# A graph network of four layers on one core: table rows two blocks later, GAT weights prepared at other places, sums of attention weights by halves

## The chip, the cores and the metric

The kernel runs on one core of a Trainium2 chip. The metric is the device time of one execution in microseconds (us), the median of three runs. The engines are called PE (TensorE, matrix products), DVE (VectorE), ACT (ScalarE), POOL (GpSimd, which here also issues the gathers) and SP (SyncE, which issues DMAs). Each engine works through its own instructions in order; semaphores hold an instruction until what it reads is there.

## What is computed

Eight batches of 2048 nodes with 128 features go through four layers. All four use the same random adjacency matrix, in which about 16 of 2048 entries of a row are set.

```python
def reference(x, adj, ...):
    x = graph_attention(adj, x, L0)     # layers 0 and 1: 8 heads of 16
    x = graph_attention(adj, x, L1)
    x = gat(x, adj, L2)                 # layers 2 and 3
    return gat(x, adj, L3)

def graph_attention(adj, h, w):
    Q, K, V = h @ Wq, h @ Wk, h @ Wv                      # per head
    attn = softmax(where(adj == 0, -inf, Q K^T / 4))
    x = layer_norm(h + (attn V) @ Wo + bo)
    return layer_norm(x + relu(x @ W1 + b1) @ W2 + b2)

def gat(x, adj, w):
    h = x @ W
    e = leaky_relu(h @ a_src [:, None] + h @ a_dst [None, :], 0.2)
    att = softmax(where(adj == 0, -inf, e))
    return layer_norm(att h + x)
```

## The kernel before

The kernel uses that the matrix is sparse. It makes a list of neighbours for each node and fetches the neighbours' rows from tables in DRAM (`tables`, one per layer; layer 0's row holds keys and values of all eight batches, 2048 numbers). Nodes are handled in 16 blocks of 128 (`NT`), one node per partition. They are sorted by their number of neighbours, so that block 0 has the fullest lists and a block needs no more slots than `CAPS` says: 28 in block 0 (and two folded ones), 23, 21 and so on down to 11 in block 15.

`start()` (L862) makes the order and layer 0's table. Its loop takes one block of 128 rows of the adjacency matrix per turn:

- `neighbours(t)` (L946): on DVE, the 2048 entries become `val`, numbers of the neighbours (L949), and 16 MAX8 instructions (L956) keep the largest eight of each segment as `cand`, which POOL writes to DRAM as `found`. On ACT, `zeros` (L941, its instruction at L944) counts the empty entries of `val`. `neighbours` returns a function, `rest`, that does the same `zeros` for `cand`. Adjacency blocks are loaded by SP, six ahead, into `adj`.
- `count(t)` (L961): DVE makes two masks from the number counted by `zeros`, and PE adds them into `places`, from which the rank of every node is known after the last block.
- `turn_x(t)` (L897): PE transposes block t of x (eight products, L329), ACT copies it (L902), and SP loads block t + 4.
- `first_rows(t)` (L905): PE multiplies the turned block with the weights (L512, 16 products), ACT copies the four results to `tops` (L518) and issues the write of 1 MB to layer 0's table (L910).
- `prepare()` (L253) is a generator that gets the weights of all layers ready, nearly all small DVE instructions, with a PE product at each `yield`. It has eight pieces: four of them belong to layers 0 and 1, the last four to layers 2 and 3 (the two GAT layers). The loop advances it by one piece per turn from t = 3 on. The small rows it works on lie in borrowed tiles (`spare`, `spare1`, from L175).

In the loop `neighbours(t)` comes first, then `count(t - 1)`, `turn_x(t + 1)`, `first_rows(t)`, `rest()`. The PSUM tiles that `turn_x` and `first_rows` share (`misc`, L103) are three in number.

After the loop DVE computes `rank` from `places` (L992 to L1010), then 16 masks `low` (L1016) and 16 small PE products (L1017) turn ranks into `perm`, the sorted order. `find_lists(0)` (L349) gathers block 0's candidates from `found` through `perm` (L352) and sorts them with MAX8 and MATCH_REPLACE8 (L362, L364) into `lists`. `fetch()` issues the first gathers of neighbours' rows (L320), 128 rows per instruction, and the first attention instruction on DVE is L606.

From then on `layers()` (L1153) sends chunks of two slots (layers 0 and 1) or four (layers 2 and 3) through stages: in layers 0 and 1 L606 multiplies keys with q, L609 sums over 16 features, ACT takes the exponential (L615), L620 multiplies the values, and PE adds the products into `acc` (L630). The weights of a block's neighbours stay in the tile `w` (partition x slot x 64 heads and batches). When a block's last chunk has its weights, `sums` calls `reciprocal_sums` (L451), which adds them over the slots (L455) and takes minimum, maximum and reciprocal. Layers 2 and 3 have eight numbers per slot instead of 64, in the PSUM tile `pair`; `gat_chunk` ends in L772.

The order of all instructions is written out by hand (`tc.manual_schedule()`): each engine executes its own in the order in which the Python code issues them.

Of the kernel before, what the change touches and what calls it, by code (L numbers as in the profile page):

```python
# [8 lines left out]
F32 = mybir.dt.float32  # L9
# [73 lines left out]
def sparse_path(ctx: ExitStack, tc: tile.TileContext, ins: dict, out: bass.AP, flag: bass.AP):  # L83
# [93 lines left out]
    def line(n):  # L177

        if spare[0] + n > NB * 2 * D:
            spare[:] = [0, work.tile([P, B, D], F32, tag="xn", name="spare1", bufs=1)]  # L180
            spare[1] = spare[1].rearrange("p b d -> p (b d)")
        spare[0] += n
        return spare[1][:1, spare[0] - n : spare[0]]

# [266 lines left out]
    def reciprocal_sums(l, t, w, columns, folded):  # L451

        sums = small.tile([P, columns], F32, tag="sums", name="sums")
        n = CAPS[t] if t > 0 else BASE
        nc.vector.tensor_reduce(  # L455
            sums, w[:, :n, :].rearrange("p s c -> p c s"), axis=AX.X, op=ALU.add
        )
        if t == 0:
            nc.vector.tensor_add(sums, sums, folded)
        nc.vector.tensor_reduce(dmin[:, l, t : t + 1], sums, axis=AX.X, op=ALU.min)  # L460
        nc.vector.tensor_reduce(dmax[:, l, t : t + 1], sums, axis=AX.X, op=ALU.max)
        nc.vector.reciprocal(sums, sums)
        return sums
# [398 lines left out]
    def start():  # L862
# [31 lines left out]
        def turned(t):  # L894
            return xTs[t % 4].rearrange("p (b n) -> p b n", n=P)

        def turn_x(t):  # L897
            if t >= NT:
                return
            xn = xs[t % 4].rearrange("p (b d) -> p b d", d=D)  # L900
            for i in range(0, B, 4):
                nc.scalar.copy(turned(t)[:, i : i + 4, :], transpose4(xn[:, i : i + 4, :]))  # L902
            load_x(t + 4)

        def first_rows(t):  # L905
            xT = turned(t)
            for i in range(0, B, 4):
                for _ in project(0, i, xT, tops[t % 2], t):
                    pass
            nc.scalar.dma_start(tables[0][t * P : (t + 1) * P, :], tops[t % 2])  # L910
# [35 lines left out]
        def neighbours(t):  # L946
            val = work.tile([P, max(CAPS), NB * NH], F32, tag="w", name="val")
            val = val.rearrange("p s c -> p (s c)").bitcast(F16)[:, :N]
            nc.vector.scalar_tensor_tensor(  # L949
                val, adj[t % 6], 0.0, iota1, op0=ALU.not_equal, op1=ALU.mult  # L950
            )
            load_adj(t + 6)
            zeros(val, none[:, t : t + 1])
            cand = work.tile([P, N // SEG, 8], F32, tag="cand", name="cand", bufs=3)
            for i in range(N // SEG):
                nc.vector.max(cand[:, i, :], val[:, i * SEG : (i + 1) * SEG])  # L956
            every = cand.rearrange("p a b -> p (a b)")
            nc.gpsimd.dma_start(found[t * P : (t + 1) * P, :], every)
            return lambda: zeros(every, left[:, t : t + 1])

        def count(t):  # L961

            d = small.tile([P, 1], F32, tag="d", name="d")
            nc.vector.tensor_scalar_max(d, none[:, t : t + 1], float(N - BINS + 1))
            nc.vector.tensor_scalar(same[:, t], falling, d, None, op0=ALU.is_equal)
            nc.vector.tensor_scalar(more[:, t], falling, d, None, op0=ALU.is_gt)
            add(ones_bf, more[:, t], 0, NT)
            add(earlier, same[:, t], t, t + 1)
            add(ones_bf, same[:, t], t + 1, NT)

        for t in range(6):
            load_adj(t)
            if t < 4:
                load_x(t)
        weights = prepare()
        for t in range(NT):
            rest = neighbours(t)
            if t > 0:
                count(t - 1)
            else:  # L980
                turn_x(0)
            turn_x(t + 1)
            first_rows(t)
            rest()
            if t >= 3:
                next(weights, None)
        for _ in weights:
            pass
        count(NT - 1)

        picked = bufs[0][:, : NT * BINS].rearrange("p (t c) -> p t c", c=BINS)
        nc.vector.tensor_mul(picked, places, same)  # L992
        rank = small.tile([P, NT], F32, tag="rank", name="rank", bufs=1)
        nc.vector.tensor_reduce(rank, picked, axis=AX.X, op=ALU.add)

# [18 lines left out]
        for t in range(NT):  # L1014
# [11 lines left out]
        nc.vector.scalar_tensor_tensor(  # L1026
            over[:, 0, :], left, float(N - N // SEG * 8), none, op0=ALU.add, op1=ALU.subtract
        )
        for i in (3, 4, 5):
            nc.scalar.copy(bufs[i], nil.to_broadcast([P, CHUNK]))  # L1030
        for l in (2, 3):
# [109 lines left out]
    def begin(c):  # L1141
        if c["l"] < 2:
            threads.append(attention_begin(c["l"], c["t"], c["box"]))
# [7 lines left out]
            next(c["run"], None)  # L1151

    def layers():  # L1153
        threads.append(find_lists(0))
        state(0, 0)
        drain()
        fetch()
        begin(every[0])
        drain()
        threads.append(find_lists(1))  # L1160
        for i in range(len(every) + 2):
# [41 lines left out]
        verdict()  # L1203
        drain()

    with tc.manual_schedule():
        start()
        layers()
# [521 lines left out]
```

## Time and profile before

| | |
|---|---|
| runs | 3429.68, 3435.26, 3435.46 us; median 3435.26 |
| profiled execution | 3404.58 us, its span 3402.8 us |
| busy, share of the span | DVE 90%, PE 81%, POOL 65%, ACT 42% |
| mean granted TensorE clock | 0.918 |
| DMA | 986.52 MB, mean 290 GB/s |
| chain that ended last | DVE 32%, PE 25%, issue 18%, DMA 10%, POOL 5%, ACT 3% |

The span goes from the first to the last instruction of one profiled execution; the execution's own time lies 1.8 us above it, and both are below the median of the runs. Busy time counts the instructions of an engine, not its waits. The profile can be asked for the instructions of an engine in order of time (start in us, duration in us, engine, line, operation, tiles, and in brackets how long the engine sat idle before and what ended that), for groups of equal instructions, for the waits between engines, and for busy times in chosen stretches. The chain that ended last is followed back from the last instruction, at each step to what released it. In the start, the stretch up to the first attention instruction at 188.62 us, the scan of block t (L949) begins at these times: 6.40, 13.66, 21.18, 31.03, 41.58, 55.03, 68.92, 79.75, 86.42, 98.20, 104.88, 117.65, 123.56, 129.45, 135.34 and 141.52 us.

### The profile page before, as it was taken

To read this page: it belongs to the slowest core of one execution; us is meant where nothing else is said; L and a number is where in the kernel's file an instruction comes from. 1 tells how busy PE (TensorE), PEld (TensorE's weight loads), DVE (VectorE), ACT (ScalarE), POOL (GpSimd) and SP (SyncE) were. 2 spreads that over 40 slices of the span, in tenths; PEclk is the share of its full clock that TensorE was granted. 3 is DMA by queue.
4 is the path that set the end of the run, shared out by engine and by line. 5 is a ranking of instruction groups with operands and counts; after the bars stand their busy time and mean duration, and the time that the engine had idled before them with its cause. 6 is when DMAs were issued, how large, how long until landed. Compare 5 with 4: busy or idle time off the path is not lost.

```text
span 3402.8 us, 34669 instructions
## 1 busy us (share of the span) xinstructions
PE 2743.1 (81%) x10618; PEld 1582.9 (47%) x10618; DVE 3058.3 (90%) x2695; ACT 1426.6 (42%) x4972; POOL 2207.9 (65%) x1453
## 2 busy tenths in 40 slices
PE   5647888878989997788888989986888976667675
PEld 4523445545555553455545555653445543233332
DVE  7789999999999999999999999976788866889885
ACT  5711333334444442233333444543555654444444
POOL 0065788588657655455676666646787865788773
PEclk9878999999999998899999999998899988888887
DMA  8587787888888777688887888767999986899883
GB/s 336 188 333 266 292 292 282 314 298 288 308 315 299 290 262 295 226 328 295 303 321 295 295 309 299 265 206 250 321 352 346 347 327 223 292 314 330 300 284 112
DMA packets 200625, 986.52 MB, mean 290 GB/s; under 512 B 31918, under 2 KB 33712, under 8 KB 128436
## 3 DMA queue, kind: packets, MB, share of 16 engines
q0 software_dynamic: 175024, 890.45, 72.4%
q1 hardware_dynamic: 20502, 75.52, 5.9%
q10 hardware_dynamic: 4904, 18.24, 1.4%
q8 instruction: 87, 1.43, 0.2%
q14 instruction: 108, 0.88, 0.1%
HBM read 937.16 MB, written 91.55 MB: 302 GB/s over the span
## 4 chain that ended last, share of the span: by engine, by line
DVE 32%; PE 25%; issue 18%; DMA 10%; POOL 5%; ACT 3%; POOLq 0%; DVEq 0%; ACTq 0%
DVE kv L620 11%; DVE kv L606 11%; PE acc L630 8%; PE acc L772 6%; DMA kv<-table,lists 4%; POOL kv L320 3%; DMA kv<-table,sorted_lists 3%; DVE sc L609 2%; PE m L712 2%; DVE kv L766 2%; DMA table<-rows,perm 2%; DVE kv L757 2%; PE m L329 2%; DVE sums L455 1%; DMA out_dram<-rows,perm 1%
## 5 line engine op out<-in xcount | busy, mean ns | idle before, releaser
L320 POOL DMA_INDIRECT kv<-table,lists x955 | 1450.0, 1518 | 357.2 <-issue 206.7
L630 PE MATMUL acc<-kv,ident 128*128 128x512 f32 x2200 | 1107.7, 634 | 222.1 <-DVE kv L620 221.9
L772 PE MATMUL acc<-kv,ident 128*128 128x512 f32 x1184 | 610.1, 667 | 188.6 <-DVE kv L766 155.4
L630 PEld LDWEIGHTS acc<-kv,ident 128*128 128x128 f32 x2200 | 413.7, 202 | 655.1 <-issue 367.5
L606 DVE TENSOR_TENSOR kv<-kv,q 128x2048 f32<-128x2048 f32 (+1 forms) x282 | 629.2, 2231 | 18.7 <-DMA kv<-table,lists 9.7
L609 DVE TENSOR_REDUCE sc<-kv 128x128 f32<-128x2048 f32 (+1 forms) x284 | 634.0, 2232 | 9.2
L620 DVE TENSOR_TENSOR kv<-kv,w 128x2048 f32<-128x2048 f32 (+1 forms) x284 | 631.4, 2223 | 4.9 <-ACT w L615 4.8
L772 PEld LDWEIGHTS acc<-kv,ident 128*128 128x128 f32 x1184 | 243.6, 215 | 504.7 <-issue 285.1
L757 DVE TENSOR_TENSOR kv<-kv,pair 128x3072 f32<-128x3072 f32 (+1 forms) x150 | 466.1, 3108 | 1.0
L476 POOL TENSOR_TENSOR rs<-ss,half 128x4 f32<-128x4 f32 x128 | 221.2, 1728 | 325.4 <-ACT n L471 324.6
L766 DVE TENSOR_TENSOR kv<-kv 128x2048 f32<-128x2048 f32 (+1 forms) x150 | 296.0, 1974 | 129.0 <-ACT kv L762 129.0
L762 ACT ACTIVATE kv<-kv,ws 128x128 f32<-128x128 f32 x1108 | 339.0, 406 | 163.7 <-DVE ws L751 105.5
L471 ACT ACTIVATE n<-m,eps 128x128 f32<-128x128 f32 x512 | 181.0, 366 | 427.1 <-PE m L712 217.4
L615 ACT ACTIVATE w<-sc,lmask 128x64 f32<-128x64 f32 x554 | 165.0, 351 | 455.3 <-DVE sc L609 454.7
L320 POOL DMA_INDIRECT kv<-table,sorted_lists x153 | 204.9, 1339 | 113.0 <-PE acc L630 41.3
L480 ACT ACTIVATE n<-m,rs 128x128 f32<-128x128 f32 x512 | 146.0, 370 | 109.4 <-POOL rs L476 109.0
L494 POOL DMA_INDIRECT table<-rows,perm x57 | 100.2, 1758 | 134.6 <-ACT rows L545 33.5
L329 PE MATMUL m<-ident,n 128*128 128x128 f32 x640 | 106.2, 288 | 73.5 <-ACT n L817 57.2
L712 PE MATMUL m<-w_L_w,hT 128*128 128x128 f32 x1024 | 156.2, 275 | 0.0
L329 PEld LDWEIGHTS m<-ident,n 128*128 128x128 f32 x640 | 82.3, 147 | 140.6 <-ACT n L817 69.0
L712 PEld LDWEIGHTS m<-w_L_w,hT 128*128 128x128 f32 x1024 | 134.9, 192 | 0.0
L691 PE MATMUL m<-n1T,w_L_gnn_W 128*128 128x512 f32 x256 | 131.5, 597 | 0.8 <-ACT n1T L686 0.4
(241 smaller groups left out, 3459.5 us busy)
## 6 DMA issues: line engine op xcount, KB each, us to landing
kept<-xT SPq DMA_DIRECT2D x48, 512.0 KB, 7.4
xT<-kept SPq DMA_DIRECT2D x48, 512.0 KB, 6.8
kv<-in_adj_dram SPq DMA_DIRECT2D x16, 1024.0 KB, 6.7
table<-kv ACTq DMA_DIRECT2D x16, 1024.0 KB, 5.0
kv<-table,lists POOLq DMA_INDIRECT x955, 7.1
kv<-in_x_nodes_dram SPq DMA_DIRECT2D x16, 512.0 KB, 5.8
kv<-table,sorted_lists POOLq DMA_INDIRECT x153, 6.3
found<-cand POOLq DMA_DIRECT2D x16, 64.0 KB, 4.0
```

The costliest lines, as they stand in the source:

```text
L320: nc.gpsimd.indirect_dma_start(out=dst, out_offset=None, in_=tables[l][:, :], in_offset=bass.IndirectOffsetOnAxis(ap=index, axis=0), bound ...
L329: nc.tensor.transpose(pt[:, j * P : (j + 1) * P], src[:, j, :], ident)
L476: nc.gpsimd.tensor_tensor(rs, ss, half[:, :4], op=ALU.pow)
L606: nc.vector.tensor_mul(kk, kk, q[:, None].to_broadcast([P, ns, NB, D]))
L609: nc.vector.tensor_reduce(sc[:, :ns].rearrange("p s (b h) -> p (s b) h", h=NH), kk.rearrange("p s b (h j) -> p (s b) h j", h=NH), axis=AX. ...
L620: nc.vector.tensor_mul(vv, vv, w[:, k : k + ns, :].rearrange("p s (b h) -> p (s b) h", h=NH)[:, :, None, :] .to_broadcast([P, ns * NB, HD, ...
L630: nc.tensor.matmul(acc[:, j, :], merge if c["folded"] else ident, kv[:, i, 4 * j : 4 * j + 4, D:], start=k + i == 0, stop=c["last"] and i ...
L712: nc.tensor.matmul(y[:, j, :], hT[:, f, j, :], wt["2"][:, f, :], start=False, stop=f == 1, skip_group_check=True,)
L757: nc.vector.tensor_mul(hv[:, :, :nv, :], hv[:, :, :nv, :], wc[:, :, :nv, None].to_broadcast([P, ns, nv, D]))
L762: nc.scalar.mul(hv[:, i, b, :], hv[:, i, b, :], ws[:, i, b - nv : b - nv + 1])
L766: nc.vector.tensor_add(hv[:, : ns - left], hv[:, : ns - left], hv[:, left:ns])
L772: nc.tensor.matmul(acc[:, j, :], merge if c["folded"] else ident, hv[:, i, 4 * j : 4 * j + 4, :], start=k + i == 0, stop=c["last"] and i = ...
```

## The change

It has three parts.

Rows of the first table come later: in turn t of the loop the kernel now turns block t - 1 (before: t + 1) and makes the table rows of block t - 2 (before: t). What is left, turning block 15 and the rows of blocks 14 and 15, follows after the loop, the rows of block 15 after DVE's first instruction on the ranks. `rest`, the counting of `cand`, is called one turn later, ahead of `turn_x`.

`prepare` is advanced in the loop only at t = 3 to 6 (layers 0 and 1). Its other pieces come at three places: one when `perm` is known, one after the gather for `find_lists(0)` has been issued, and the rest after the first gathers of neighbours' rows have been issued. `find_lists(0)` is therefore called in `start()` instead of `layers()`, and the borrowed tile `spare1` is that of `hT` instead of that of `xn`.

In layers 0 and 1 the sum over the slots is no longer one reduction: the upper half of the slots is added to the lower half, in place in `w`, until two are left, and these are added into `sums`.

```diff
     def line(n):
         if spare[0] + n > NB * 2 * D:
-            spare[:] = [0, work.tile([P, B, D], F32, tag="xn", name="spare1", bufs=1)]
-            spare[1] = spare[1].rearrange("p b d -> p (b d)")
+            spare[:] = [0, work.tile([P, 2, 4, P], F32, tag="hT", name="spare1", bufs=1)]
+            spare[1] = spare[1].rearrange("p f b c -> p (f b c)")
...
         n = CAPS[t] if t > 0 else BASE
-        nc.vector.tensor_reduce(
-            sums, w[:, :n, :].rearrange("p s c -> p c s"), axis=AX.X, op=ALU.add
-        )
+        if l < 2:
+            while n > 2:
+                m = -(-n // 2)
+                nc.vector.tensor_add(w[:, : n - m, :], w[:, : n - m, :], w[:, m:n, :])
+                n = m
+            nc.vector.tensor_add(sums, w[:, 0, :], w[:, 1, :])
+        else:
+            nc.vector.tensor_reduce(
+                sums, w[:, :n, :].rearrange("p s c -> p c s"), axis=AX.X, op=ALU.add
+            )
...
         def turn_x(t):
-            if t >= NT:
+            if t < 0:
                 return
...
         def first_rows(t):
+            if t < 0:
+                return
...
-        weights = prepare()
+        rest = None
         for t in range(NT):
-            rest = neighbours(t)
+            now_rest = neighbours(t)
             if t > 0:
                 count(t - 1)
-            else:
-                turn_x(0)
-            turn_x(t + 1)
-            first_rows(t)
-            rest()
-            if t >= 3:
+                rest()
+            rest = now_rest
+            turn_x(t - 1)
+            first_rows(t - 2)
+            if 3 <= t < 7:
                 next(weights, None)
-        for _ in weights:
-            pass
         count(NT - 1)
+        rest()
+        turn_x(NT - 1)
+        first_rows(NT - 2)

         picked = bufs[0][:, : NT * BINS].rearrange("p (t c) -> p t c", c=BINS)
         nc.vector.tensor_mul(picked, places, same)
+        first_rows(NT - 1)
...
             over[:, 0, :], left, float(N - N // SEG * 8), none, op0=ALU.add, op1=ALU.subtract
         )
+        next(weights, None)
+        threads.append(find_lists(0))
+        advance(threads)
+        next(weights, None)
...
     def layers():
-        threads.append(find_lists(0))
         state(0, 0)
         drain()
         fetch()
         begin(every[0])
+        for _ in weights:
+            pass
         drain()
...
+    weights = prepare()
     with tc.manual_schedule():
         start()
         layers()
```

## The prediction

> **What bounds the kernel.** The page names VectorE (DVE): busy 90% of the span. That is an average, so I cut the span by stage. In layers 0 and 1 (about 188 to 2240 us) the windows view leaves DVE almost no gap, and the waits view puts all of DVE's idle time there at 30 us. Columns: stretch, length, then busy us with instruction counts for PE, weight loads, DVE, ACT, POOL, then clock, DMA share, GB/s.
>
> ```profile
> 300.00:500.00 200.00, 161.26 (x583) 91.48 (x584) 197.61 (x134) 61.84 (x210) 143.56 (x84) 0.91 0.78 285
> 1900.00:2100.00 200.00, 183.05 (x830) 113.96 (x829) 197.54 (x101) 84.26 (x306) 131.02 (x73) 0.97 0.82 304
> ```
>
> So in those layers DVE work saved is time saved. The start (0 to 188 us) is different, and I read it in the timeline, engine by engine. DVE's gaps stand in brackets:
>
> ```profile
> 30.54 0.15 DVE L964 TENSOR_SCALAR d<-none 128x1 f32<-128x1 f32 x1 [3.85 <-ACT junk L944]
> ...
> 155.09 0.15 DVE L964 TENSOR_SCALAR d<-none 128x1 f32<-128x1 f32 x1 [6.45 <-ACT junk L944]
> ...
> 157.21 1.22 DVE L992 TENSOR_TENSOR kv<-places,same 128x1024 f32<-128x1024 f32 x1 [1.54 <-PE places L926]
> ...
> 173.32 0.29 DVE L362 MAX8 top<-cand 128x8 f32<-128x128 f32 x1 [7.45 <-DMA cand<-found,perm]
> ...
> 188.62 2.29 DVE L606 TENSOR_TENSOR kv<-kv,q 128x2048 f32<-128x2048 f32 x1 [9.75 <-DMA kv<-table,lists]
> ```
>
> Late in the loop DVE waits for ACT's `zeros` of the block just scanned, and ACT is late because it copies rows before it. After the loop DVE waits twice for gathers, 7.45 and 9.75 us, with nothing to do. ACT's own rows for one late block:
>
> ```profile
> 138.38 0.40 ACT L944 ACTIVATE junk<-cand,onesc 128x128 bf16<-128x128 f32 x1 [0.40 <-ACT kv L518]
> ...
> 138.91 2.00 ACT L944 ACTIVATE junk<-val,onesc 128x2048 bf16<-128x2048 f16 x1
> ...
> 140.91 1.05 ACT L902 COPY kv<-m 128x512 f32<-128x512 f32 x2
> ...
> 145.41 0.40 ACT L944 ACTIVATE junk<-cand,onesc 128x128 bf16<-128x128 f32 x1 [0.41 <-ACT kv L518]
> ```
>
> From one `cand` row to the next, **7.03 us per block** on ACT: 0.53 + 2.00 + 0.94 + four row copies paced by PE at 0.86 to 0.98 (3.18) + 0.38 for issuing the table write. DVE's block (L949 to L949, 129.45 to 135.34) takes **5.89 us** without weights. The weights of `prepare`, advanced once per block at t = 3 to 10, add on DVE, start to start: 3.5, 4.9, 8.0, 4.9 for layers 0 and 1, then 0.8, 5.2, 0.8, 5.2 for layers 2 and 3, 33.3 us in all.
>
> **Rows two blocks behind, and GAT weights out of the loop.** These two act on one schedule, so I run it once, with the durations above. Until 18.48 us nothing changes: ACT issues its weight loads, loads a table, and starts the first `zeros` at 18.48; DVE's first `count` ends at 21.18. Then ACT's second `zeros` comes directly (ended by 22.5), not behind two turned blocks and four row copies, so the 3.85 us gap goes and block 3's scan starts at 21.18 + 5.89 = 27.1 (before: 31.03). Each later scan start adds 5.89 and the weights that stay: block 4 at 36.5, 5 at 47.3, 6 at 61.2, 7 at 72.0 (before 79.75). The 2.52 us wait for a PE product at 50.09 goes, since the product then has some 2 us to spare. No weights follow, so the count after block 7's scan ends at 77.9.
>
> From there ACT is the slower one. For that block PE needs 1.2 (places) + 1.04 (turning) + 3.5 (row products) after the count, ACT one copy and the issue more: 77.9 + 6.9 = 84.8. Eight blocks remain: block 15's `zeros` starts at 84.8 + 7 x 7.03 = 134.0 and ends at 136.0, against 154.96 in the trace: **19 us gained**, 11.9 of them from weights taken out of the loop.
>
> The lag must be paid at the end. Before block 15's places, PE still has row products of block 13 (3.5) behind ACT's 0.5 for `cand`, then 1.0 for the places: DVE multiplies `picked` at 141.1, against 157.21, **16 gained**. Next the changed order puts the turning of block 15 and the rows of 14 and 15 on PE: 1.04 + 3.5 + 3.5 = 8.0 us, to 149.1. DVE's ranking (157.21 to 162.06, 4.85 us) used to reach its 16 small products with PE free; now they **wait some 3 us** behind those rows, because `first_rows(NT - 1)` is issued before them. With the row of 3.0 to 3.3 us for the 16, `perm` is out at 152.7 against 165.79: 13 gained. In the blocks 3 to 7 PE has gaps, and the windows at 70 to 80 and 100 to 110 show a clock of 0.66 in such stretches (eight transposes 1.9 instead of 1.04 us at 124.82), which would delay block 7 by 1 to 2 us. I take **12 us**; bounds 7 (three slow blocks more on PE) and 17 (the 16 products find PE free).
>
> What moves with it: the 12 x-loads after the first four go out two blocks later and sit in SP's queue before the adjacency load of the next block; that load is six blocks ahead, so a few us of delay reach nobody. The 16 table writes (1 MB each, about 5 us to land) are issued later on ACT's queue; the last leaves at about 150 and lands near 155, the first gather of its rows starts at about 167. ACT's clearing of three buffers (10.76 us) ends near 161 instead of 168.9, and the x-gather it must precede lands near 163: 2 us of slack instead of 7.7. POOL's order of gathers stays.
>
> **GAT weights in the waits.** The 0.8 goes ahead of the gather's wait, the first 5.2 into it: DVE is free from about 152.8, does 0.8, waits about 0.7 for PE's one-column products (round trip as at 177.24 to 177.97) and 5.2, done at about 159.5; the lists land at 153.5 + 6.7 = 160.2. **Slack 0.7 us**, so this costs nothing or a little. The other 0.8 + 5.2 run while the first rows are gathered: 165.9 to 172.7, against a landing near 175.6. PE's q products stand behind one such product, 2 us later than before, and q has 6 us of slack (182.46 against 188.62). If the covers failed, all 11.9 us would be back.
>
> **Sums by halves.** One strided reduction per block becomes 4 or 5 in-place additions, twice 16 blocks. DVE's groups by form (count, then busy us and mean ns):
>
> ```profile
> L455 DVE TENSOR_REDUCE sums<-w 128x64 f32<-128x1792 f32 x2 | 6.3, 3145 | 0.0
> L455 DVE TENSOR_REDUCE sums<-w 128x64 f32<-128x1152 f32 x4 | 8.5, 2122 | 0.0
> L455 DVE TENSOR_REDUCE sums<-w 128x64 f32<-128x704 f32 x2 | 2.7, 1372 | 3.4 <-ACT w L615 3.4
> ```
>
> The thirteen forms sum to 64.7 us, about 1.65 ns an element beyond a fixed part. The additions: 28 slots go 14, 7, 3, 2, 1 times 64 elements; over all blocks 72 additions and 16576 elements per layer. Price from rows of contiguous fp32 TENSOR_TENSOR: 276 ns for 128 elements, 542 for 384, 1218 for 1024, so 143 ns + 1.04 ns an element. Sum: 2 x (72 x 0.143 + 16576 x 0.00104) = 55.1 us. Dependent neighbours leave 0.035 us more (40.05 + 0.27, next at 40.35), on 112 more instructions 3.9. **64.7 - 55.1 - 3.9 = 5.7 us saved.** For 11 slots nothing is won; for 28, 0.5 us each. Bounds: 9.6 (no gaps) and 0 (0.05 us more per addition, were rows of 64 elements dearer: L459's 226 ns against 210 by the line).
>
> Here a rule speaks against the change. The Trainium skill, "VectorE: DVE Perf Modes", has tensor_reduce and fp32 tensor_tensor both at 1x in "The perf-mode tier table", gives (N + 151)/0.96 ns for the addition under "The TRN2 errata", and advises under "Rules for kernel authors" to minimise the count of chained operations. For additions the formula holds here (2291 ns for 2048; the trace has 2284). Giving the reduction the same rate, 32 x 0.157 + 35200/960 = 41.7 us against 144 x 0.157 + 33152/960 = 57.2: **15.5 us lost**. But the row for 1792 strided elements is 3145 ns where that rate makes 2024. The same page calls tensor_reduce the slowest operation, without a figure for the stride. The row decides: 5.7 us gained. DVE's busy share in these layers lets 5 of it through.
>
> **The sum.** 12 + 5.5 = 17.5 us off the profiled execution: 3404.6 (span 3402.8 and 1.8 around it) to 3387. That execution lies 0.9% below the median of the runs, 3435.26, so I carry the difference: **3417.8 us**.
>
> **Rivals.**
> 1. *The forecast*, 0.70: start 7 to 17, sums 0 to 9, so 3409 to 3428.
> 2. *The gain goes further*, 0.06: both upper bounds, 3435.3 - 26.6 = 3409 and below, if PE is warm and the places are never late.
> 3. *The weights are not hidden*, 0.12: the slack of 0.7 us is thin and each part needs a product from PE. All 11.9 us come back: 3435.3 - 0.1 - 5.5 = 3430. Against it: waits of 7.45 and 9.75 us stand in the trace, and only 6 us go into each.
> 4. *The additions cost what the rule says*, 0.05: 3435.3 - 12 + 15.5 = 3439. Against it: the rows of L455.
> 5. *Slower by PE's clock*, 0.07: PE holds 25% of the chain of waits, 850 us, at a mean granted clock of 0.918. With unchanged cycles each 0.01 of clock lost costs about 9.3 us, in the sums into `acc` of L772 above all (6% of the chain, in layers 2 and 3, where the windows show 0.84 to 0.94). From 0.019 lost it outweighs the gain; at 0.03 it is 3435.3 - 17.5 + 28 = 3446. For it: the clock wanders between 0.79 and 1.00 from stage to stage. Against it: no instruction of those layers changes, they only begin earlier.
>
> What a measurement of this kernel can tell is about 0.2%, 7 us. Faster by more: 0.80 (the forecast, 2, and the better part of 3); within: 0.12; slower: 0.08. Range: 3409 to 3428, 3 us for the spread of the runs, and upward over rival 3: **3404 to 3434**.
>
> **What would show it.** Start: the ACT wait of 3.85 us near 30 gone; block 15's scan near 120 to 125 instead of 141.52; the last `zeros` of `val` ending near 136; the 16 L1017 products starting with PE just off L512, after DVE's ranking; the gap before the first MAX8 of the lists shrinking from 7.45 to about 1 and the one before the first L606 from 9.75 to about 3; that first L606 near 176. Sums: 144 additions at L455's place, near 55 us busy, and DVE's 30 us of idle in layers 0 and 1 not grown. Wrong would be: `perm` later than 160 (the tail eats the gain), the first L606 later than 180 with weights directly ahead of it, additions above 65 us, or layers 2 and 3 longer than the 1150 us or so they take now.

## The result and the profile after

| | before | after |
|---|---|---|
| median of 10 runs, us | 3435.36 | 3420.66 |
| lowest to highest, us | 3429.62 to 3441.48 | 3417.85 to 3428.05 |
| ratio | | 0.9965, 95% interval 0.9955 to 0.9975 |
| profiled execution, its span, us | 3404.58, 3402.8 | 3428.05, 3426.3 |

The kernel is **faster by 0.35%**, 12 us by the ratio (8.6 to 15.5 by its interval) and 14.7 us between the medians; 3417.8 was forecast.

The two spans can't be subtracted: the profiled execution of before lies 31 us under the median of the runs it stands beside here, and that of after has a stretch in layer 2 (2480 to 2620 us, granted clock 0.79 to 0.87 and 280 to 309 GB/s, where before shows 0.89 to 0.96 and 345 to 350) that takes some 26 us longer. It makes layers 2 and 3 longer than before, which the prediction had named as a sign of being wrong, but it did not come back when the kernel ran again (experiment 4). So I compare by stages. The start first, in the timeline of VectorE (DVE) of after; the columns are as before, and the lines have moved by 8 to 12 (L606 is now L614, L620 is L628, L992 is L1003, L1016 is L1028).

```profile
139.39 0.15 DVE L974 TENSOR_SCALAR d<-none 128x1 f32<-128x1 f32 x1 [7.88 <-ACT junk L954]
...
143.77 1.23 DVE L1003 TENSOR_TENSOR kv<-places,same 128x1024 f32<-128x1024 f32 x1 [3.80 <-PE places L936]
...
151.69 2.42 DVE L1028 TENSOR_SCALAR low<-iota,lo 128x128 bf16<-128x128 f16 x13 [2.51 <-PE m L1029]
...
154.61 0.17 DVE L1035 TENSOR_TENSOR perm<-part,m 128x16 int32<-128x16 f32 x1
...
163.02 0.29 DVE L362 MAX8 top<-cand 128x8 f32<-128x128 f32 x1 [1.70 <-DMA cand<-found,perm]
...
179.17 2.29 DVE L614 TENSOR_TENSOR kv<-kv,q 128x2048 f32<-128x2048 f32 x1 [2.77 <-DMA kv<-table,lists]
```

The reader is to see four things. The last count comes 15.7 us earlier (139.39 against 155.09), but between it and `perm` stand two waits for PE: 3.80 (it was 1.54) and 2.51, which is new. So `perm` is 11.0 us earlier (154.61 against 165.62). The two waits for gathers have shrunk from 7.45 and 9.75 us to 1.70 and 2.77: the weights of layers 2 and 3 now stand in them. And the first attention instruction comes at 179.17 instead of 188.62, 9.5 us earlier.

The sums, in DVE's groups by form (count, then busy us and mean ns):

```profile
L461 DVE TENSOR_TENSOR sums<-w 128x64 f32<-128x64 f32 x32 | 7.3, 229 | 1.1
L459 DVE TENSOR_TENSOR w<-w 128x128 f32<-128x128 f32 x24 | 7.1, 294 | 0.8
...
L459 DVE TENSOR_TENSOR w<-w 128x896 f32<-128x896 f32 x2 | 2.2, 1082 | 0.0
```

All forms together are 144 instructions and 57.4 us, where 64.7 us of reductions stood. Taken from the first instruction of each sum to the minimum behind it, 32 sums took 66.4 us before and 62.7 in the kernels with halves (measured in experiments 2 and 4): **3.7 us less on DVE**.

As a third view I compare the times at which block t's minimum is taken, layer by layer. After stands 9.9 us ahead of before at the first block of layer 0, 9.0 at the last one, and only 4.9 at the first block of layer 1. Something takes 4 us back between layers 0 and 1. And DVE waits more: between the first attention instruction and the last sum of layer 1 its gaps come to 20.4 us before and 28.0 after (27.0 in experiment 4).

### The profile page after: what moved, and what is told of

Same layout as the page of the kernel before. It is cut to its first block, busy times and chain, and to the rows that moved or that the text cites. A ratio compares the mean times of both kernels' runs of the same rounds, so it can differ in the third digit from the quotient of the medians.

```text
span 3426.3 us, 34767 instructions
## 1 busy us (share of the span) xinstructions
PE 2761.3 (81%) x10618; PEld 1595.4 (47%) x10618; DVE 3051.6 (89%) x2807; ACT 1425.1 (42%) x4972; POOL 2229.1 (65%) x1453
## 4 chain that ended last, share of the span: by engine, by line
DVE 36%; PE 23%; issue 19%; DMA 11%; POOL 4%; ACT 4%; POOLq 0%; ACTq 0%; DVEq 0%; another core or an unknown queue 0%
DVE kv L614 13%; DVE kv L628 13%; PE acc L780 7%; PE acc L638 5%; DMA kv<-table,lists 4%; POOL kv L320 3%; DVE sc L617 3%; DMA kv<-table,sorted_lists 2%; DVE kv L774 2%; PE m L329 2%; DVE kv L765 2%; DMA table<-rows,perm 1%; DMA xs<-in_x_nodes_dram,perm 1%; PE m L720 1%; DVE w L459 1%
## 5 line engine op out<-in xcount | busy, mean ns | idle before, releaser
L628 DVE TENSOR_TENSOR kv<-kv,w 128x2048 f32<-128x2048 f32 (+1 forms) x284 | 631.5, 2223 | 8.6 <-ACT w L623 7.9
L614 DVE TENSOR_TENSOR kv<-kv,q 128x2048 f32<-128x2048 f32 (+1 forms) x282 | 629.2, 2231 | 10.7 <-DMA kv<-table,sorted_lists 5.7
```

The costliest lines, as they stand in the source:

```text
L614: nc.vector.tensor_mul(kk, kk, q[:, None].to_broadcast([P, ns, NB, D]))
L628: nc.vector.tensor_mul(vv, vv, w[:, k : k + ns, :].rearrange("p s (b h) -> p (s b) h", h=NH)[:, :, None, :] .to_broadcast([P, ns * NB, HD, ...
```

## The experiments

Each kernel was timed against the kernel before on one chip; before had medians of 3405 to 3409 us there, so ratios are what can be compared across batches. The changed kernel itself ran again as experiment 4.

### 1 to 4: the start alone, the sums alone, the sums twice, all again

Experiment 1 is the changed kernel with the reduction of before in `reciprocal_sums`; 2 is the kernel before with only that function changed; 3 is the kernel before with every reduction of layers 0 and 1 made a second time, over the same numbers in dense order, its result unused (its diff below); 4 is the changed kernel.

```diff
+        if l < 2:
+            dense = small.tile([P, columns], F32, tag="dense", name="dense", bufs=1)
+            flat = w[:, :n, :].rearrange("p s c -> p (s c)")
+            nc.vector.tensor_reduce(
+                dense, flat.rearrange("p (c s) -> p c s", s=n), axis=AX.X, op=ALU.add
+            )
```

> The rows two blocks later and the GAT weights in the waits, with the sums as one reduction as before. Theory A (the start gave nearly the whole gain, the sums little): the first product of layer 0 (first instruction on kv with q) again near 179 us, and 10 to 12 us below the kernel before (ratio about 0.9967). Theory B (half of the start's gain is lost again at the layers' boundaries and the sums make up for it): 5 us or less (0.9985).

> The sums by halves alone, the start as before. Theory A (the additions save what their rows say, 64.7 - 57.4 - 3.9 us of chaining = 3.4 us): 2 to 5 us below before (ratio about 0.999). Theory B (chained additions hold up DVE and give the saving back): no difference or slower, 0 to +5 us. If the forecast's 5.7 us were right: 0.9983.

> Before, with a second reduction beside each of the 32 in layers 0 and 1: over the same numbers and as many, but read in order in memory, into a tile that nobody reads. Two questions. The price of the stride: if one number per DVE cycle is the rate without it, 1792 numbers take about 2.0 us against 3.15, and all 32 take about 42 us against 64.7; if the stride costs nothing, 3.1 us and 65. What a us of DVE is worth in these layers: if all of it reaches the end, the kernel is slower by the added busy time (42 us, 1.2%); if only half, 21 us.

> The changed kernel once more, for a second trace. Theory A (the profiled execution of the changed kernel was 23 us longer than that of the kernel before by a slow stretch of layer 2 that either kernel falls into or not, not by the change): ratio again 0.9955 to 0.9975, the start and layers 0 and 1 within 1 us of the first trace, and blocks 5 to 8 of layer 2 may differ by up to 25 us. Theory B (the change brings the slow stretch about): blocks 5 to 8 of layer 2 slow again, by the same 25 to 27 us against the trace of before.

| | median us | ratio to before, 95% interval |
|---|---|---|
| 1, start only | 3392.48 | 0.9964, 0.9953 to 0.9976 |
| 2, sums only | 3404.62 | 0.9998, 0.9988 to 1.0008 |
| 3, sums twice | 3440.5 | 1.0104, 1.0089 to 1.0120 |
| 4, all | 3392.1 | 0.9958, 0.9945 to 0.9972 |

The start brings the whole gain, and the sums bring nothing that can be measured: by the interval of experiment 2 they are worth between 4.1 us gained and 2.7 us lost, so the forecast of 5.5 us is out, and 3 us is not. Experiment 3 gives two prices. Two forms of its groups, strided and dense reductions of the same count:

```profile
L455 DVE TENSOR_REDUCE sums<-w 128x64 f32<-128x1792 f32 x2 | 6.3, 3148 | 0.0
...
L461 DVE TENSOR_REDUCE dense<-w 128x64 f32<-128x1792 f32 x2 | 4.0, 2006 | 0.0
```

The stride of 64 numbers costs a reduction 1.57 times the time of a dense one (3148 against 2006 ns). So the weighing of rule and row in the prediction was right: the rule's rate for the reduction holds, but for dense reading only (2024 ns by the rule, 2006 measured). And 41 us of added DVE work cost 35 us of time, about 85% (74 to 100% by the interval). By that, 3.7 us less on DVE should give some 3 us, which is at the edge of what these intervals can show.

### Where the gain of the sums goes

The traces show two places. One is layer 0. DVE's waits between the sums of its blocks 0 and 15 come to 6.7 to 8.0 us in the six kernels with halves (2, 4, 7, 8, 11 and after) and to 4.6 to 6.2 in five with the reduction (before, 1, 5, 6 and 10), so layer 0's half of the saving is waited away: the stretch takes 925.5 to 927.0 us with halves and 924.9 to 926.5 without. In layer 1 the saving comes through: from the sum of block 0 to that of block 14 it is 809.3 to 810.1 us with halves and 810.8 to 811.5 without.

The larger loss sits at the boundary of layers 0 and 1. There POOL issues the write of block 15's rows into layer 1's table (before and after it POOL waits), and layer 1's first gathers wait for it. The kernel before, then experiment 2, POOL's timeline:

```profile
1261.97 1.06 POOL L494 DMA_INDIRECT table<-rows,perm  x1 [7.93 <-issue]
```

```profile
1263.34 3.16 POOL L502 DMA_INDIRECT table<-rows,perm  x1 [8.11 <-issue]
```

The same instruction takes 1.06 us in one and 3.16 in the other. DVE's timeline beside it tells why; before, then experiment 2:

```profile
1259.89 2.29 DVE L609 TENSOR_REDUCE sc<-kv 128x128 f32<-128x2048 f32 x1
1262.10 2.28 DVE L620 TENSOR_TENSOR kv<-kv,w 128x2048 f32<-128x2048 f32 x1
...
1273.02 2.29 DVE L620 TENSOR_TENSOR kv<-kv,w 128x2048 f32<-128x2048 f32 x1 [3.26 <-ACT w L615]
```

```profile
1261.09 2.29 DVE L617 TENSOR_REDUCE sc<-kv 128x128 f32<-128x2048 f32 x1
1263.29 2.28 DVE L628 TENSOR_TENSOR kv<-kv,w 128x2048 f32<-128x2048 f32 x1
...
1276.52 2.29 DVE L628 TENSOR_TENSOR kv<-kv,w 128x2048 f32<-128x2048 f32 x1 [5.40 <-ACT w L623]
```

Before, the write starts 0.13 us ahead of the multiplication, still inside the reduction, which has one input. In experiment 2 it starts 0.05 us inside the multiplication, which reads two. It then lasts 0.9 us beyond that instruction's end, lands 6.8 us after its start instead of 4.6, and POOL's next gather comes 2.1 us later, counted from the start of the write. DVE waits 5.40 us afterwards instead of 3.26. PE, idle for 4.49 us instead of 2.34, then runs at a granted clock of 0.50 (1275 to 1280 us; 1.00 at that place before), and four products into `acc` take 3.62 us instead of 1.88. Behind it DVE has two more waits, 1.78 us for ACT and 0.66 for PE, that before does not have.

One case is no rule, so I counted POOL's 298 indirect transfers (gathers and writes of rows) in layer 0 of the kernel before (400 to 1200 us) by the DVE instruction in which each started. In the reduction L609: 98 of 98 took 1.06 us or less. In the two multiplications: 149 of 154 took more than 1.5 us, with medians of 2.87 (L620) and 1.91 (L606). In all others, 46, they took 1.06 us or less; four of these started in a multiplication that reads one input from PSUM (L643). The Trainium skill, "SBUF — State Buffer", says under "Who interferes with whom" that a DVE instruction with two SBUF inputs contends with a POOL instruction that reads SBUF, and that one with at most one SBUF input (outside modes that use both ports) does not. The counts agree. In two points the page and the runs differ, and the measurement decides. The same list tells of a probe in which a `tensor_tensor` did not stall a DMA, with a reason that it calls inferred; here it holds up POOL's transfers. And it says that whichever issues first has the shared port for the whole of its instruction while the other is blocked; here that shows in one direction only, since 86 multiplications that began while a transfer was under way took 2.28 us, like the other 123.

The rule was left out of the prediction. Directly the additions matter little by it: 35 transfers of layers 0 and 1 that started in one in the kernel after took 1.08 us at the median and 1.74 at most.

But which kernel meets the long write is chance. In the ten kernels compared below it starts 35.5 to 36.0 us behind the last sum of layer 0, and a shift of 0.2 us decides. Experiment 6, described below, has the reduction of before, and its write is long (POOL, then DVE):

```profile
1255.40 3.11 POOL L494 DMA_INDIRECT table<-rows,perm  x1 [8.17 <-issue]
```

```profile
1255.29 2.28 DVE L620 TENSOR_TENSOR kv<-kv,w 128x2048 f32<-128x2048 f32 x1
...
1268.52 2.29 DVE L620 TENSOR_TENSOR kv<-kv,w 128x2048 f32<-128x2048 f32 x1 [5.17 <-ACT w L615]
```

Experiment 7, also below, has the halves, and its write is short:

```profile
1254.28 1.06 POOL L502 DMA_INDIRECT table<-rows,perm  x1 [7.93 <-issue]
```

```profile
1254.40 2.28 DVE L628 TENSOR_TENSOR kv<-kv,w 128x2048 f32<-128x2048 f32 x1
...
1265.60 2.29 DVE L628 TENSOR_TENSOR kv<-kv,w 128x2048 f32<-128x2048 f32 x1 [3.23 <-ACT w L623]
```

From the last sum of layer 0 to the first of layer 1 it is 156.4 to 156.8 us in the four kernels with a short write and nothing added there (before, 1, 5 with the reduction, 7 with halves) and 160.3 to 161.2 in the six with a long one (6 and 10 with the reduction; 2, 4, 11 and after with halves). So the 3.5 to 4.4 us go with the write and not with the sums.

Comparing like with like, from the first attention instruction to the last sum of layer 1, the halves are ahead by 1 to 4 us among the kernels with the long write (2052.0 to 2053.5 us against 2054.3 and 2055.9), and not ahead among those with the short one (2050.5 against 2049.0 to 2051.9). What they are worth by themselves stays open between nothing and some 3 us.

### 8: two short one-input instructions at that place

Added to the changed kernel:

```diff
+            if i == 147:
+                gap = small.tile([P, 1], F32, tag="late", name="gap", bufs=1)
+                nc.vector.tensor_reduce(gap, ident[:, :128], axis=AX.X, op=ALU.max)
+                nc.vector.tensor_reduce(gap, ident[:, :128], axis=AX.X, op=ALU.max)
             go(c1, 2)
```

> The kernel after, with two added one-input reductions of 128 numbers (about 0.4 us together, results unused) on DVE just ahead of the multiplication by the weights of chunk 146 (layer 1, slots 8 and 9 of block 0, near 1251 us), nothing else. Theory (a two-input DVE instruction holds up POOL's issue of an indirect transfer that starts inside it): the scatter of block 15's rows, which started 0.07 us inside that multiplication, now starts inside the added reductions and takes 1.06 instead of 3.15 us; the gathers of layer 1's first re-sorted lists start 2 us earlier, the wait for ACT w behind them shrinks from about 7 to about 3.4 us, and the kernel, though it does 0.4 us more, is 2.5 to 4 us below after (near 3389). Rival (the long transfer is due to something else, such as the state of the queue or the landing of the gathers): scatter stays near 3.1 us and the time is equal or 0.4 us longer.

POOL's timeline, then DVE's:

```profile
1251.57 1.06 POOL L502 DMA_INDIRECT table<-rows,perm  x1 [8.01 <-issue]
```

```profile
1249.41 2.29 DVE L617 TENSOR_REDUCE sc<-kv 128x128 f32<-128x2048 f32 x1
1251.62 0.28 DVE L1218 TENSOR_REDUCE gap<-ident 128x1 f32<-128x128 f32 x1
1251.93 0.29 DVE L1219 TENSOR_REDUCE gap<-ident 128x1 f32<-128x128 f32 x1
1252.13 2.28 DVE L628 TENSOR_TENSOR kv<-kv,w 128x2048 f32<-128x2048 f32 x1
...
1262.63 2.29 DVE L628 TENSOR_TENSOR kv<-kv,w 128x2048 f32<-128x2048 f32 x1 [3.42 <-ACT w L623]
```

The write is back at 1.06 us and the wait at 3.42 (5.04 in experiment 4). From the last block of layer 0 to the first of layer 1 this kernel loses 1.8 us on before, 0.5 of it its own added work; experiment 4 loses 4.4. So 2.5 us came back, the lower end of what was expected. Two reservations: here the write started 0.05 us before the added instructions, inside the last of the reduction, so this trace does not show what it would have done without them; and the time, 3392.43 (ratio 0.9953, 0.9939 to 0.9968), can't be told from experiment 4's. The mechanism is shown by the count and by the ten traces of this boundary named above; its worth in time is read from traces only.

### 5 and 6: rows alone, weights alone

Both have the reduction of before. Experiment 5 has rows two blocks behind but leaves the weights in the loop; 6 moves the weights but not the rows.

Experiment 5 against the changed kernel (its reduction is left out here), then experiment 6 against the kernel before (the tile of `spare1` is left out):

```diff
-            if 3 <= t < 7:
+            if 3 <= t:
                 next(weights, None)
...
-        next(weights, None)
         threads.append(find_lists(0))
         advance(threads)
-        next(weights, None)
```

```diff
-            if t >= 3:
+            if 3 <= t < 7:
                 next(weights, None)
-        for _ in weights:
-            pass
...
+        next(weights, None)
+        threads.append(find_lists(0))
+        advance(threads)
+        next(weights, None)
...
-        threads.append(find_lists(0))
...
         begin(every[0])
+        for _ in weights:
+            pass
```

> The rows two blocks behind and the first gather of found numbers put ahead, but the weights of layers 2 and 3 stay in the loop (one step per block from t = 3 on) and the sums are the reductions of before. My schedule of the prediction, run with 11.9 us of weights in blocks 7 to 10 on DVE: the last zeros of val ends near 145 (before 155, after 135), perm near 159 to 161 (before 165.6, after 154.6), so 5 to 7 us below the time of before; against start-only (-12.4 us) 5 to 7 us are missing and belong to the weights. Rival (the slower engine of the loop is ACT, and DVE's slack takes the weights in): perm near 155 and the full 11 to 12 us below before.

> Rows stay one block ahead of the neighbours' second half as before, only the weights of layers 2 and 3 leave the loop for the waits behind perm; sums are reductions. If ACT sets the loop of before from block 8 on (7.03 us a block, 13 us behind DVE at the end), DVE's 11.9 us taken out bring little: perm near 161 to 165, time 1 to 5 us below before. If DVE sets it in blocks 7 to 10, some 8 to 12 us. The two parts add up to -12.4 us only if they act on different stretches; if e5 and e6 together give clearly less, the gain needs both.

| | last count | `perm` minus count | first attention instruction | ratio, 95% interval |
|---|---|---|---|---|
| before | 155.09 | 10.5 | 188.62 | |
| 5, rows | 147.93 | 15.2 | 187.13 | 0.9991, 0.9985 to 0.9998 |
| 6, weights | 147.12 | 10.5 | 180.69 | 0.9969, 0.9957 to 0.9980 |
| 1, both | 137.44 | 15.2 | 177.45 | 0.9964, 0.9953 to 0.9976 |

The **weights do most of it** (7.9 us at the first attention instruction), the rows little (1.5), both 11.2. For the rows alone 5 to 7 us were expected; for the weights the second of the two cases came true. In the loop each part gains as much as the other, 7.2 and 8.0, and together 17.7. But the rows pay 4.7 us back behind the loop, where two blocks of rows stand on PE:

```profile
152.30 1.23 DVE L995 TENSOR_TENSOR kv<-places,same 128x1024 f32<-128x1024 f32 x1 [3.80 <-PE places L928]
...
160.24 2.42 DVE L1020 TENSOR_SCALAR low<-iota,lo 128x128 bf16<-128x128 f16 x13 [2.51 <-PE m L1021]
```

This is the timeline of experiment 5. The first wait was 1.54 us before, the second did not exist: 2.3 + 2.5. In experiment 6 both are as before.

### 7 and 10: the rows of block 15 later

The new wait of 2.51 us is in front of the ranking's products. Experiment 7 is the changed kernel with `first_rows(NT - 1)` behind `perm`; 10 is experiment 1 with it behind the first gather and one step of the weights as well, as this diff has it:

```diff
         nc.vector.tensor_mul(picked, places, same)
-        first_rows(NT - 1)
...
         threads.append(find_lists(0))
         advance(threads)
         next(weights, None)
+        first_rows(NT - 1)
```

> The kernel after, with the rows of block 15 (its products on PE, copies on ACT, its table write) put behind perm instead of between picked and rank. If the new wait of 2.5 us before the second of the 16 products of the ranking is those rows standing on PE, it goes, perm comes 2 to 2.5 us earlier (near 152.3), and the time is 2 to 2.5 us below after (3390). Rival: the wait is for the products' own round trip from DVE to PE at a low clock, then perm stays within 0.5 us and the time too. A third way: the rows then stand on PE and ACT in front of the weights and the first q, the first multiplication by q starts no earlier, time equal or 1 to 2 us above after.

> Start-only with the rows of block 15 put behind perm, the first gather of found numbers and the second step of the weights, so that the ranking's products do not stand behind them and neither do the products of that step. Theory: perm at about 150 as with rows15_late, the lists land near 158.7, weights end before 159, first multiplication by q near 175, some 2 us below start-only (about 3390 against 3392.5). Rival: the later steps of the weights or the own-number products stand behind those rows on PE instead, or the late table write holds up the first gathers: no gain.

The wait goes in both: from the last count to `perm` 12.7 us instead of 15.2. The time does not follow: ratios 0.9961 (0.9946 to 0.9976) and 0.9961 (0.9949 to 0.9973). In experiment 7 the weights wait 4.31 us for a product behind those rows. In 10 they wait 0.69, and the lists still come no sooner; here DVE's timeline of 10:

```profile
144.42 1.23 DVE L995 TENSOR_TENSOR kv<-places,same 128x1024 f32<-128x1024 f32 x1 [3.80 <-PE places L928]
...
152.50 0.17 DVE L1025 COPY part<-m 128x16 f32<-128x16 f32 x1 [0.28 <-PE m L1020]
...
163.72 0.29 DVE L362 MAX8 top<-cand 128x8 f32<-128x128 f32 x1 [4.02 <-DMA cand<-found,perm]
```

The gather was issued at 153.73 and took 10.0 us to land, not 6.7. What stays the same is another distance, from the write of the ranks (`ranks`, 8 KB in about 2,000 packets of 4 bytes, issued by SP just before the ranking): 16.2 to 16.9 us to the landing in experiments 1, 4, 5, 7, 8, 9 and 10 and in after, whatever `perm` did. In the kernel before and in 2, 3 and 6 it was 13.1 to 13.6 us. The difference goes with a table write of 1 MB that ACT issues 2.55 us behind the ranks in the first eight and not in the other four. That write is held up too: it takes 12.6 to 13.7 us to land (in the eight traces with the write that show it: 1, 4, 5 and 7 to 11), where one issued 2.35 us ahead of the ranks takes 4.0 in before. So the next limit behind `perm` is in the DMA queues; experiment 12 takes that write away.

### 12: both blocks' rows behind the gather, and a partial move of the sums to PE

> Start-only with two changes in separate stretches, told apart by the trace. First, the rows of blocks 14 and 15 both go behind the first gather of found numbers and one step of the weights. Theory from the runs so far: with perm 2.5 us earlier the gather still landed 16.8 us after the write of the ranks, because those 2048 packets of 4 bytes and the gather shared the DMA engines with the two 1-MB table writes of these blocks (13.6 us in the kernel before); without them ahead of it perm comes near 148, the lists near 155 to 156, the first multiplication by q near 172 to 174 instead of 177.5, 3 to 5 us gained. Rival: the table writes or the rows' products on PE then stand in front of the weights, the lists or the first gathers of the table, and 177 to 180 stays. Second, sums on PE only for the blocks with many slots (4 to 7 of layer 0, 2 to 7 of layer 1), where PE has some 7 us of idle time in a block, read three slots later so that DVE does not wait for PE at the block's end (71 us of waiting when all blocks did it); other blocks keep the reduction. If so, some 2 us off DVE in each of 10 blocks and 8 to 19 us off the time; rival: PE still sets the pace of these blocks, and nothing or a loss of up to 20 us. Both theories together: 11 to 24 us below start-only, near 3368 to 3381 where before is 3405.

Against experiment 1, its first part:

```diff
         turn_x(NT - 1)
-        first_rows(NT - 2)
...
         threads.append(find_lists(0))
         advance(threads)
         next(weights, None)
+        first_rows(NT - 2)
+        first_rows(NT - 1)
```

Its first part is read from the start of its trace. With no table write between ranks and gather, the gather (issued at 153.57) lands 6.6 us later, 13.5 after the ranks, and the first table write behind it takes 3.9 us: the 10.0 and 16.8 came with the table write. But then the rows stand in front of q:

```profile
160.15 0.29 DVE L362 MAX8 top<-cand 128x8 f32<-128x128 f32 x1 [0.61 <-DMA cand<-found,perm]
...
182.02 2.29 DVE L616 TENSOR_TENSOR kv<-kv,q 128x2048 f32<-128x2048 f32 x1 [8.08 <-ACT q L594]
```

The first attention instruction comes at 182.02, 4.6 us later than in experiment 1. Of these, 2.3 were lost in the loop already, whose last count is at 139.77 instead of 137.44. From that count it is 42.3 us, against 38.4 to 40.0 in experiments 1, 4, 8 and 9 (39.1 in 10). So three places were tried for this PE work, and each put it before something that is needed: a product for the weights in 7, q in 10 and 12.

### 9 and the second part of 12: sums on PE

Experiment 9 takes the sums off DVE: for each chunk PE adds the weights of its two slots into PSUM, and one short reduction of two halves stays. Blocks 0 and 1 of layer 1, whose chunks alternate, keep the reduction. Against the changed kernel:

```diff
+            nc.tensor.matmul(
+                halves(t)[:, : ns * NB * NH], ident,
+                w[:, k : k + ns, :].rearrange("p s c -> p (s c)"),
+                start=k == 0, stop=c["last"], skip_group_check=True,
+            )
...
-                nc.vector.tensor_add(w[:, : n - m, :], w[:, : n - m, :], w[:, m:n, :])
+            nc.vector.tensor_reduce(
+                sums, halves(t).rearrange("p (s c) -> p c s", s=2), axis=AX.X, op=ALU.add
+            )
```

> The kernel after, but the sums of layers 0 and 1 (blocks 0 and 1 of layer 1 excepted, which keep the reduction) are made on PE: one product of identity with the two slots of weights of a chunk (128 columns, 254 in all), added up in PSUM, and at the end of the block one reduction over two halves on DVE. By DVE alone: 57 us of additions go, some 30 short reductions (0.25 us) and two long ones (4.7 us) come, so some 45 us off VectorE, which at the 0.85 us of time per us of DVE that the doubled sums showed is 35 to 40 us below after (near 3355). By PE: 254 products of 0.28 us add 70 us to a PE that was busy 88% of layers 0 and 1; rival: PE or the gathers set the pace then and the gain is 0 to 20 us, with DVE waiting for acc at each block's end.

The time is **above that of before**, which neither expectation had: ratio 1.0063 (1.0050 to 1.0076). One group of PE and one of DVE:

```profile
L641 PE MATMUL pair<-w,ident 128*128 128x128 f32 x486 | 95.8, 280 | 0.0
...
L463 DVE TENSOR_REDUCE sums<-pair 128x64 f32<-128x128 f32 x30 | 8.7, 290 | 70.7 <-PE pair L641 70.7
```

Each fp32 product is two records in the profile (512 with the 26 of 64 columns, for 256 products), so PE took 100 us and not my 70, and DVE stood 70.7 us before 30 reductions. DVE's share of 98% in layer 0 of the changed kernel hid that PE, at 88% in the same stretch, is close behind.

In experiment 12 only blocks 4 to 7 of layer 0 and 2 to 7 of layer 1 have it, and the reduction comes three slots later. Its ratio is 0.9971 (0.9961 to 0.9980), no better than experiment 1, where 11 to 24 us less were expected. By the block times it lost 10 us on experiment 1 in layer 0 and won 7.9 in layer 1. In layer 0 DVE waited 11.9 us for ACT's `w` before its multiplications, and 1.6 us in the kernel before. A version with the six blocks of layer 1 alone was not tried.

### 11: the weights in one piece

Against the changed kernel:

```diff
-        next(weights, None)
+        for _ in weights:
+            pass
         threads.append(find_lists(0))
         advance(threads)
-        next(weights, None)
```

> The kernel after, with all remaining weights of layers 2 and 3 made before the first gather of found numbers, behind perm, where nothing covers them. If they are hidden in after, this costs what they take: 0.8 + 5.2 + 0.8 + 5.2 us and their round trips to PE, about 12 to 13 us later at the first multiplication by q and in the time. Rival: part of it is covered anyway or was not hidden in after; 4 to 8 us.

The ratio is 0.9982 (0.9974 to 0.9990), some 6 to 8 us above experiments 1 and 4, and the first attention instruction comes at 181.40, 29.0 us behind `perm`; in experiments 1, 8 and 9 it is 23.1 to 24.8. So having 12 us of weights together costs 4 to 6 us at that place. They were not without cover, as I had written: POOL issued the gather at 153.40 all the same, 1.0 us behind `perm`, and its 7 us hid the first half; the second half stuck out. In after, DVE still waits 1.70 and 2.77 us for the transfers behind each half, so there both are hidden. What 12 us without any cover cost was not tried.

## Why the prediction was right

- **The time**: 3417.8 forecast, 3420.66 measured. The forecast was 17.5 us down, 12 from the start and 5.5 from the sums; the start gave 12.3 (experiment 1, by its ratio), the sums nothing measurable. By the ratio the gain is 12 us, short of the forecast by what the sums were to bring; that the medians lie 14.7 us apart, and the forecast only 3 us off, is partly luck.
- **The loop**: 19 us forecast for the last `zeros`, 15.7 in the profile and 17.7 in experiment 1. In the profiled execution twelve row products took 4.28 us instead of 2.86 (131.96 us), at a granted clock of 0.65 instead of 1.00 in experiment 1: the slow PE that the lower bound was for. "11.9 of them from weights" was mis-sized: moving the weights alone gives 8.0, the rows alone 7.2, together 2.5 more than their sum.
- **The lag paid at the end**: 19 less 13, 6 us, forecast; 4.7 measured. The new wait was forecast at 3 us and is 2.51. `perm` came 11.0 us earlier (13.0 in experiment 1), with 13 in the schedule and 12 taken.
- **The weights in the waits**: the slack was forecast at 0.7 us and is 1.70, with a gather that took 7.4 us instead of the 6.7 reckoned with; where it took 6.2 and 6.6 (experiments 6 and 12) the slack is 0.2 and 0.6. Rival 3 is out. That a table write behind the ranks is held up, and the gather with it, the prediction did not see: it let every table write land in about 5 us. The gap before the first attention instruction is 2.77, forecast 3; the instruction came at 179.17 instead of 176 (176.9 to 177.0 in experiments 4, 8 and 9).
- **The sums**, the step that failed: "DVE's busy share in these layers lets 5 of it through" (the forecast then took 5.5). Of 5.7 us forecast on DVE 3.7 came: the additions took 57.4 us and not 55.1, since those of 64 to 128 numbers are some 20 ns above my line (294 ns for 128, 276 taken), while the gaps between them came as forecast (3.6 us, 3.9 taken). Then these 3.7 were spent, in layer 0 on waits for ACT and PE (1.4 us of it at the end of the two blocks with 14 slots in experiment 4), and at the boundary of the layers, where 3.5 to 4.4 us were lost to the long write. The first goes with the halves in six traces; why DVE's waits grow there was not followed further. The second is chance. The 30 us of idle time on which the step rested include the 9.75 before the first attention instruction; the rest was 20.4 and grew to 28.0. And the prediction left out that DVE's instructions can hold up POOL.
- **Rule against row** (15.5 us lost or 5.7 won): the row was the right guide; rival 4 is out, by experiment 2.
- **PE's clock**, rival 5: in the same batch 0.916 to 0.923 in experiment 1 and 0.919 to 0.924 in experiment 4, against 0.915 to 0.921 before. It did not fall. (The ten runs of the result, 0.909 to 0.918, have no clocks of before beside them.)

## What to carry to other kernels

Where an engine stands idle for a transfer, small work that must be done anyway can be hidden there: moving 12 us of weight preparation out of the loop into two waits brought 8 us. Work shifted out of a loop comes due at its end, so count the queue behind it (4.7 of 7.2 us here), and look for the next limit, since removing that queue moved nothing. And a saving of a few us on the busy engine can be lost, or won, by chance: here a transfer of GpSimd that starts 0.2 us later, inside a two-input instruction of VectorE instead of a one-input one, costs some 4 us. Before a small difference is put down to a change, look for the same loss in kernels without it.

## What the runs showed of the hardware

- An indirect transfer issued by POOL took 1.06 us or less if it started in a one-input reduction of DVE (98 of 98), and over 1.5 us if it started in a multiplication with two inputs in SBUF (149 of 154; up to 3.16 in experiment 2). The multiplications were not slowed by transfers already under way (2.28 us, 86 of them).
- A reduction whose inner stride is 64 fp32 numbers took 1.57 times a dense one (3148 and 2006 ns for 1792 numbers).
- A write of 8 KB in packets of 4 bytes took 12.5 to 13.4 us to land. A write of 1 MB issued 2.55 us behind it took 12.6 to 13.7 us instead of 4.0, and with that one a gather issued 7 to 9 us behind the small packets landed 16.2 to 16.9 us after them, against 13.1 to 13.6 without.
